# Quantizing, a norm and decay products spread over ScalarE and GpSimd in an attention, conditioning and quantized FFN kernel

## The chip, the cores and the metric

The kernel runs on one core of a Trainium2 chip. The metric is the device time in microseconds (us) of one execution. TensorE is written PE in the profile (its weight loads PEld), VectorE DVE, ScalarE ACT, GpSimd POOL and SyncE SP.

## The reference

The input x has 8 batches of 512 tokens with 256 channels, in fp32. Two blocks follow each other, both with a residual:

```python
x = x + attn(cond(x, itok), ...)
x = x + ffn(cond2(x, ...), w_gate, w_up, w_down)
```

- cond picks one of eight weight matrices per batch and applies it.
- attn is causal linear attention with 16 heads (no softmax), a gate and a layer norm.
- cond2 has a recurrence over time (causal_ema), a gate, eight decaying traces of the gated input with learned rates, which are blended, a second gate, and then the norm that this change touches:

```python
out = einsum(soma * gate, Wout)
mu, var = out.mean(-1), out.var(-1)
return (out - mu) / sqrt(var + 1e-5) * gamma + beta
```

- ffn quantizes its inputs per token to 8 bits before each of its products, and its weights to three values:

```python
scale = 127.0 / clip(max(abs(x), axis=-1), 1e-5)
xq = clip(round(x * scale), -128, 127) / scale
```

  It does this to the output of cond2 (256 channels) and to silu(gate) * up (1024 channels).

## The kernel before

**Stages.** For each batch there are three generators: attention(b), cond2(b) and ffn(b). A token tile has 128 tokens, so a batch has NT = 4 of them; C = 256 channels are KC = 2 blocks of 128. Each generator stops at yields. The list at the end of the kernel (L786 to L810) gives each a start and a step: attention b starts at b with steps of 1/14, cond2 at b + 4/3 with steps of 1/10, ffn at b + 8/3 with steps of 1/9. The part with the lowest time is traced next. So in the middle of the run, attention of one batch is interleaved with cond2 of the one or two before it and with ffn of the two or three before it. At the end only cond2 and ffn, then only ffn are left.

**Order on an engine.** The kernel is traced by the Tile framework. It gives every instruction a rank by its place in the traced program, adds the waits that data and buffers need, and decides when the kernel is built, from estimates of its own, in which order each engine gets its instructions. On the chip each engine takes its instructions in that order.

**Buffers.** A pool has a number of buffers per tag (bufs); a tile of the same tag takes the next. The function bank() at L57 hands out the PSUM banks of pool ps: four buffers, one bank each, used by nearly every product outside the attention's energies and outputs, which have pools ps_e and ps_o.

**cond2 (L555 to L685).** It transposes the attention's result (px2T, L562), makes soma, h1 and mod (L567 to L590), the gated input (L593 to L609), and the traces in four parts of two decays each (L631 to L655). Each part makes dm, the decay table times mod, on GpSimd with one instruction per token tile (L634 to L637), multiplies it with gated on TensorE into ptr (L646), and adds the results to tempT on VectorE (L652). At L665 to L685 the product with woutT goes to a bank pw (two token tiles in each), ScalarE copies it to c2 (L674), VectorE takes mean and variance of each token (L675, layer_stats), GpSimd makes 1/sqrt(var + 4 eps) (L677, layer_rstd, with a power at L186), and VectorE applies mean and gamma (L679), then 1/sqrt and beta (L682). (The factor 4: gate is kept as 1 + tanh, twice the sigmoid, and the norm takes the factor out.)

**ffn (L726 to L781).** VectorE takes the largest absolute value amax of c2 (L731), and brings c2 to its quantized form: it multiplies by inv and adds MAGIC = 1.5 x 2^23, which rounds to an integer (L738), and subtracts MAGIC again on the way to bf16 (L739, tile cq). TensorE transposes cq (L743) and ScalarE copies it out (cqT). Then, per token tile, TensorE makes gate and up in two halves of 512 (L756), ScalarE the silu (L759), VectorE the product h (L760). After a yield VectorE takes hmax (L763), h_inv and hstep (L721, L723, L766), scales and rounds h in the same two steps (L767, L769, tile hq); TensorE transposes hq (phq, L772), ScalarE copies it out (hqT, L774), TensorE multiplies with w_downT (pd, L777), VectorE adds the residual (res, L779), and SyncE's queue writes it out (L780).

Of the kernel before, what the change touches and what calls it, by code (L numbers as in the profile page):

```python
# [8 lines left out]
F32 = mybir.dt.float32  # L9
BF = mybir.dt.bfloat16  # L10
I32 = mybir.dt.int32
AF = mybir.ActivationFunctionType
ALU = mybir.AluOpType
AX = mybir.AxisListType

P = 128
EPS = 1e-5

MAGIC = 12582912.0
# [13 lines left out]
def adaln_attn_ffn_kernel(ctx: ExitStack, tc: tile.TileContext, a: dict, out: bass.AP):  # L33
    nc = tc.nc
    x = a["x"]
    B, T, C = x.shape
    NT = T // P
    KC = C // P
# [8 lines left out]
    cp = ctx.enter_context(tc.tile_pool(name="const", bufs=1))  # L47
# [3 lines left out]
    p1 = ctx.enter_context(tc.tile_pool(name="p1", bufs=1))  # L51
    p2 = ctx.enter_context(tc.tile_pool(name="p2", bufs=2))
# [13 lines left out]
    nc.vector.memset(ones, 1.0)  # L66
    minus_half = cp.tile([P, 1], F32, name="minus_half")
    nc.vector.memset(minus_half, -0.5)

    causal = cp.tile([P, 64], F32, name="causal")  # L70
    for r in range(2):
# [35 lines left out]
    def load_w(name, src, pool=cp, tag=None, eng=nc.scalar):  # L107
        rows, cols = src.shape
        t = pool.tile([P, rows // P, cols], F32, tag=tag or name, name=name)
        eng.dma_start(t, src.rearrange("(k p) n -> p k n", p=P))  # L110
        return t
# [25 lines left out]
    def chunk(t):  # L137
        return slice(t * P, (t + 1) * P)
# [38 lines left out]
    def layer_stats(src, mv_row):  # L177
        st = p3.tile([P, nc.vector.BN_STATS_DIM], F32, tag="bn", name="bn")
        nc.vector.bn_stats(st, src)
        nc.vector.bn_aggr(mv_row, st)  # L180

    def layer_rstd(mv, name):

        r = p2.tile([P, NT], F32, tag="rstd", name=name)
        nc.gpsimd.tensor_scalar(r, mv[:, :, 1], 4.0 * EPS, None, ALU.add)
        nc.gpsimd.tensor_tensor(r, r, minus_half.to_broadcast([P, NT]), ALU.pow)  # L186
        return r
# [235 lines left out]
    w = {}  # L423

    def setup_cond2():
        for n in ("wgT", "wn1T", "wsomaT", "wtempT", "woutT"):
            w[n] = load_w(n, a[n], eng=nc.gpsimd)
        for n in ("bg", "gamma_c", "beta_c"):
            w[n] = load_row(n, a[n])

# [124 lines left out]
    def cond2(b):  # L555
# [29 lines left out]
        mod = p2.tile([P, NT, D], F32, tag="mod", name=f"mod_{b}")  # L585
# [45 lines left out]
        for d in range(0, D, 2):  # L631

            dm = p2.tile([P, NT, 2, 64], F32, tag="dm", name=f"dm_{b}_{d}")
            for t in range(NT):  # L634
                nc.gpsimd.tensor_mul(  # L635
                    dm[:, t], w["decay"][:, d : d + 2], mod[:, t, d : d + 2].unsqueeze(2).to_broadcast([P, 2, 64])
                )  # L637
            for k in range(KC):

                ptr = [  # L640
                    bank(f"ptr_{b}_{k}_{d}_{r}").rearrange("p (e t n) -> p e t n", e=2, n=64) for r in range(2)
                ]
                for t in range(NT):
                    for r in range(2):
                        rows = slice(64 * r, 64 * (r + 1))
                        nc.tensor.matmul(  # L646
                            ptr[r][:, :, t, :], gated[rows, t, chunk(k)], dm[rows, t], start=True, stop=True
                        )
                for r in range(2):
                    acc = tempT[:, k, :].rearrange("p (t r n) -> p t r n", r=2, n=64)[:, :, r, :]  # L650
                    for e in range(2):
                        nc.vector.scalar_tensor_tensor(  # L652
                            acc, ptr[r][:, e], w["bw_c"][:, k, d + e : d + e + 1], acc, ALU.mult, ALU.add
                        )
            yield  # L655
# [7 lines left out]
            nc.vector.scalar_tensor_tensor(soma[:, o, :], gate, 1.0, soma[:, o, :], ALU.add, ALU.mult)  # L663
        yield
        c2 = p1.tile([P, NT, C], F32, tag="c2", name=f"c2_{b}")  # L665
        mv = p2.tile([P, NT, 2], F32, tag="mvc", name=f"mvc_{b}")
        for t in range(0, NT, 2):
            pw = bank(f"pwo_{b}_{t}").rearrange("p (t c) -> p t c", t=2)
            for u in range(2):
                for k in range(KC):  # L670
                    nc.tensor.matmul(
                        pw[:, u, :], soma[:, k, chunk(t + u)], w["woutT"][:, k, :], start=k == 0, stop=k == KC - 1
                    )
            nc.scalar.copy(c2[:, t : t + 2, :], pw)  # L674
            for u in range(2):  # L675
                layer_stats(c2[:, t + u, :], mv[:, t + u, :])
        rstd = layer_rstd(mv, f"rstd_c{b}")  # L677
        for t in range(NT):
            nc.vector.scalar_tensor_tensor(  # L679
                c2[:, t, :], c2[:, t, :], mv[:, t, 0:1], w["gamma_c"], ALU.subtract, ALU.mult  # L680
            )
            nc.vector.scalar_tensor_tensor(  # L682
                c2[:, t, :], c2[:, t, :], rstd[:, t : t + 1], w["beta_c"], ALU.mult, ALU.add
            )
        c2s[b] = c2  # L685


# [38 lines left out]
    def ffn(b):  # L726
        c2, x2 = c2s[b], x2s[b]


        amax = p2.tile([P, NT], F32, tag="amax", name=f"amax_{b}")  # L730
        nc.vector.tensor_reduce(amax, c2, AX.X, ALU.max, apply_absolute_value=True)  # L731
        inv = act_scales(amax, [P, NT], f"c_inv_{b}")
        steps = p2.tile([P, 2, NT], F32, tag="steps", name=f"steps_{b}")
        for i in range(2):
            nc.vector.tensor_scalar(steps[:, i, :], amax, w["wstep"][:, i : i + 1], None, ALU.mult)
        cq = p1.tile([P, NT, C], BF, tag="cq", name=f"cq_{b}")
        for t in range(NT):
            nc.vector.tensor_scalar(c2[:, t, :], c2[:, t, :], inv[:, t : t + 1], MAGIC, ALU.mult, ALU.add)  # L738
        nc.vector.tensor_scalar(cq, c2, -MAGIC, None, ALU.add)  # L739
        pt = bank(f"pcq_{b}", BF).rearrange("p (k n) -> p k n", k=KC)  # L740
        for k in range(KC):
            for t in range(NT):
                nc.tensor.transpose(pt[:, k, chunk(t)], cq[:, t, chunk(k)], ident_bf)  # L743
        cqT = p2.tile([P, KC, T], BF, tag="cqT", name=f"cqT_{b}")
        nc.scalar.copy(cqT, pt)
        yield

        for t in range(NT):
            h = p2.tile([P, INNER], F32, tag="h", name=f"h_{b}_{t}")
            for j in range(INNER // 512):  # L750
                cols = slice(j * 512, (j + 1) * 512)
                pgu = []
                for n in ("w_gateT", "w_upT"):
                    pm = bank(f"p{n}_{b}_{t}_{j}")
                    for k in range(KC):
                        nc.tensor.matmul(pm, cqT[:, k, chunk(t)], w[n][:, k, cols], start=k == 0, stop=k == KC - 1)  # L756
                    pgu.append(pm)
                sig = p2.tile([P, 512], F32, tag="sig", name=f"sig_{b}_{t}_{j}")
                nc.scalar.activation(sig, pgu[0], AF.Silu, scale=steps[:, 0, t : t + 1])  # L759
                nc.vector.scalar_tensor_tensor(h[:, cols], pgu[1], steps[:, 1, t : t + 1], sig, ALU.mult, ALU.mult)  # L760
            yield
            hmax = p2.tile([P, 1], F32, tag="hmax", name=f"hmax_{b}_{t}")
            nc.vector.tensor_reduce(hmax, h, AX.X, ALU.max, apply_absolute_value=True)  # L763
            hinv = act_scales(hmax, [P, 1], f"h_inv_{b}_{t}")
            hstep = p2.tile([P, 1], F32, tag="hstep", name=f"hstep_{b}_{t}")
            nc.vector.tensor_scalar(hstep, hmax, w["wstep"][:, 2:3], None, ALU.mult)  # L766
            nc.vector.tensor_scalar(h, h, hinv, MAGIC, ALU.mult, ALU.add)  # L767
            hq = p2.tile([P, INNER], BF, tag="hq", name=f"hq_{b}_{t}")
            nc.vector.tensor_scalar(hq, h, -MAGIC, None, ALU.add)  # L769
            pt = bank(f"phq_{b}_{t}", BF)  # L770
            for k in range(KI):
                nc.tensor.transpose(pt[:, chunk(k)], hq[:, chunk(k)], ident_bf)  # L772
            hqT = p2.tile([P, INNER], BF, tag="hqT", name=f"hqT_{b}_{t}")
            nc.scalar.copy(hqT, pt)  # L774
            pd = bank(f"pd_{b}_{t}")[:, :C]
            for k in range(KI):
                nc.tensor.matmul(pd, hqT[:, chunk(k)], w["w_downT"][:, k, :], start=k == 0, stop=k == KI - 1)  # L777
            res = p2.tile([P, C], F32, tag="res", name=f"res_{b}_{t}")
            nc.vector.scalar_tensor_tensor(res, pd, hstep, x2[:, t, :], ALU.mult, ALU.add)  # L779
            nc.sync.dma_start(out[b, chunk(t), :], res)  # L780
            yield  # L781
# [12 lines left out]
    while line:  # L794
        line.sort()
        at, step, b, what = line.pop(0)
# [73 lines left out]
```

## Time and profile before

| | |
|---|---|
| Time, median of three runs | 1080.57 us (1074.35 to 1085.64) |
| Profiled execution, its own time | 1082.68 us |
| Its span, first to last instruction | 1080.9 us |
| Mean granted TensorE clock | 0.88 of full speed |
| Busy: TensorE, VectorE, ScalarE, GpSimd | 849.7, 565.6, 300.9, 252.2 us |
| VectorE busy in 597 to 716 (one batch, in the middle) | 62.4 of 119 us |
| VectorE busy in 910 to 1030 (cond2 and ffn left) | 80.1 of 120 us |
| VectorE: L763, L767, L769, 32 each | 1218, 869, 755 ns |
| VectorE: L679, L682, 32 each | 471, 667 ns |
| GpSimd: dm (L635), 128 | 411 ns |

The profile shows one execution. Busy is the time in which an engine had an instruction under way. A line of the waits reads: engine, tile and line that waited, the engine, tile and line that released it, then the total in us, how often, and the longest. A line of the order of time reads: start and duration in us, engine, line, operation, written tile<-read tiles, shapes, count, and in brackets how long the engine sat idle before it and what ended that.

### The profile page before, as it was taken

To read this page: it belongs to the slowest core of one execution; us is meant where nothing else is said; L and a number is where in the kernel's file an instruction comes from. 1 tells how busy PE (TensorE), PEld (TensorE's weight loads), DVE (VectorE), ACT (ScalarE), POOL (GpSimd) and SP (SyncE) were. 2 spreads that over 40 slices of the span, in tenths; PEclk is the share of its full clock that TensorE was granted. 3 is DMA by queue.
4 is the path that set the end of the run, shared out by engine and by line. 5 is a ranking of instruction groups with operands and counts; after the bars stand their busy time and mean duration, and the time that the engine had idled before them with its cause. 6 is when DMAs were issued, how large, how long until landed. Compare 5 with 4: busy or idle time off the path is not lost.

```text
span 1080.9 us, 22096 instructions
## 1 busy us (share of the span) xinstructions
PE 849.7 (79%) x9644; PEld 573.9 (53%) x9644; DVE 565.6 (52%) x1231; ACT 300.9 (28%) x481; POOL 252.2 (23%) x379
## 2 busy tenths in 40 slices
PE   1789679799778996799968996899778995885654
PEld 0466547566555674566735674566555674543322
DVE  8724534435552845537462736446543547656743
ACT  1832131223222231234222331234122421331221
POOL 6443222223122211222123211133122211011000
PEclk9899779798986898998988998899988998888866
DMA  9000110000000000000100000000000000000000
GB/s 282 12 3 12 41 39 2 11 1 2 2 15 6 7 26 5 16 6 2 26 15 6 7 26 5 16 1 7 25 6 5 7 7 6 10 5 6 10 10 15
DMA packets 16850, 19.31 MB, mean 18 GB/s; under 512 B 3330, under 2 KB 15394, under 8 KB 16754
## 3 DMA queue, kind: packets, MB, share of 16 engines
q1 hardware_dynamic: 12418, 10.56, 3.2%
q0 software_dynamic: 2048, 5.58, 1.6%
q10 hardware_dynamic: 2288, 1.76, 0.5%
q8 instruction: 76, 1.25, 0.5%
q14 instruction: 20, 0.16, 0.1%
HBM read 13.63 MB, written 4.19 MB: 16 GB/s over the span
## 4 chain that ended last, share of the span: by engine, by line
PE 50%; DVE 18%; issue 14%; POOL 9%; ACT 8%; DMA 1%; ACTq 0%; POOLq 0%; DVEq 0%
PE po L315 6%; PE pwg L598 5%; PE pe L297 4%; DVE tempT L652 4%; POOL ktok L235 4%; PE pd L777 3%; PE ptr L646 3%; PE pso L579 3%; PE py L203 3%; PE pw_gateT L756 2%; DVE hmax L763 2%; POOL st L268 2%; PE ptg L660 2%; ACT sig L759 2%; PE phq L772 2%
## 5 line engine op out<-in xcount | busy, mean ns | idle before, releaser
L652 DVE SCALAR_TENSOR_TENSOR tempT<-ptr,bw_c,tempT 128x256 f32<-128x256 f32 x256 | 104.6, 475 | 45.4 <-PE ptr L646 45.2
L760 DVE SCALAR_TENSOR_TENSOR h<-pw_upT,steps,sig 128x512 f32<-128x512 f32 x64 | 47.2, 748 | 112.8 <-ACT sig L759 67.8
L646 PE MATMUL ptr<-dm,gated 64*128 64x128 f32 x1024 | 94.8, 319 | 7.7 <-DVE tempT L652 7.0
L646 PEld LDWEIGHTS ptr<-dm,gated 64*128 64x128 f32 x1024 | 85.2, 222 | 23.3 <-issue 19.7
L772 PE MATMUL phq<-ident_bf,hq 128*128 128x128 bf16 x256 | 26.0, 262 | 83.2 <-DVE hq L769 83.2
L216 PE MATMUL pkq<-wkq,yT 128*128 128x512 f32 x128 | 78.2, 740 | 16.2 <-DVE tempT L652 10.5
L235 POOL TENSOR_TENSOR ktok<-sg,cs 128x512 f32<-128x512 f32 x32 | 42.2, 1319 | 177.9 <-ACT sg L223 177.9
L297 PEld LDWEIGHTS pe<-qT,kT 32*64 32x64 f32 x2048 | 66.6, 136 | 29.8 <-issue 24.5
L297 PE MATMUL pe<-qT,kT 32*64 32x64 f32 x2048 | 80.2, 228 | 0.9 <-ACT qT L243 0.9
L774 ACT COPY hqT<-phq 128x1024 bf16<-128x1024 bf16 x32 | 32.4, 1013 | 156.2 <-PE phq L772 156.2
L635 POOL TENSOR_TENSOR dm<-decay,mod 128x128 f32<-128x128 f32 x128 | 48.5, 411 | 98.5 <-PE ptr L646 98.5
L772 PEld LDWEIGHTS <-hq 128*128 128x128 bf16 x256 | 20.4, 118 | 90.6 <-DVE hq L769 89.2
L777 PE MATMUL pd<-w_downT,hqT 128*128 128x256 bf16 x256 | 46.1, 341 | 19.9 <-ACT hqT L774 19.5
L759 ACT ACTIVATE sig<-pw_gateT,steps 128x512 f32<-128x512 f32 x64 | 43.2, 686 | 66.5 <-PE pw_gateT L756 65.4
L301 DVE TENSOR_TENSOR et<-pe,causal 128x512 f32<-128x512 f32 x64 | 43.8, 687 | 33.1 <-PE pe L297 32.4
L779 DVE SCALAR_TENSOR_TENSOR res<-pd,hstep,x 128x256 f32<-128x256 f32 x32 | 15.4, 481 | 87.3 <-PE pd L777 87.3
L223 ACT ACTIVATE sg<-pkq 128x512 f32<-128x512 f32 x32 | 19.1, 597 | 117.5 <-PE pkq L216 117.5
L216 PEld LDWEIGHTS pkq<-wkq,yT 128*128 128x128 f32 x128 | 26.1, 226 | 41.3 <-issue 28.7
L242 PE MATMUL pkT<-ident,ktok 128*128 128x128 f32 x128 | 21.1, 287 | 33.8 <-POOL ktok L235 33.8
L756 PEld LDWEIGHTS <-cqT 128*128 128x128 bf16 x256 | 24.5, 104 | 42.7 <-issue 20.2
L756 PE MATMUL pw_gateT<-w_gateT,cqT 128*128 128x512 bf16 x128 | 41.9, 412 | 5.9 <-ACT sig L759 2.4
L268 POOL TENSOR_TENSOR st<-total,own 128x256 f32<-128x256 f32 x56 | 40.6, 749 | 23.4 <-DVE total L278 17.5
(222 smaller groups left out, 1610.9 us busy)
## 6 DMA issues: line engine op xcount, KB each, us to landing
x<-in_x_dram SPq DMA_DIRECT2D x8, 512.0 KB
out_dram<-res SPq DMA_DIRECT2D x32, 128.0 KB
wt<-in_weightT_dram SPq DMA_DIRECT2D x8, 256.0 KB
bw<-in_blend_dram POOLq DMA_DIRECT2D x2, 512.0 KB, 6.1
w_gateT_raw<-in_w_gateT_dram POOLq DMA_DIRECT2D x2, 512.0 KB, 7.3
w_upT_raw<-in_w_upT_dram POOLq DMA_DIRECT2D x2, 512.0 KB, 4.2
w_downT_raw<-in_w_downT_dram POOLq DMA_DIRECT2D x2, 512.0 KB, 4.7
wgT<-in_wgT_dram POOLq DMA_DIRECT2D x1, 512.0 KB, 6.8
```

The costliest lines, as they stand in the source:

```text
L216: nc.tensor.matmul(pkq, yT[:, k, chunk(t)], wkq[:, k].rearrange("p e c -> p (e c)"), start=k == 0, stop=k == KC - 1)
L235: nc.gpsimd.tensor_mul(tok.rearrange("p (h e d) -> p h e d", e=2, d=HD), sg[:, i].unsqueeze(2).to_broadcast([P, H, 2, HD]), cs[:, t, :].re ...
L268: nc.gpsimd.tensor_mul(sts[c], total[0].rearrange("p (g f) -> p g f", g=NG).unsqueeze(2).to_broadcast([P, NG, 2, 2 * HD]), own.rearrange(" ...
L297: nc.tensor.matmul(pe[64 * r : 64 * (r + 1), g, u, :], kT[rows, g, at], qT[rows, g, at], start=True, stop=True)
L315: nc.tensor.matmul(po[q : q + 32, r, half, u, :], *factors, start=(r, q) not in begun, stop=last)
L598: nc.tensor.matmul(pwg[:, u, :], src[:, k % KC, chunk(t + u)], w["wgT"][:, k, :], start=k == 0, stop=k == 2 * KC - 1,)
L646: nc.tensor.matmul(ptr[r][:, :, t, :], gated[rows, t, chunk(k)], dm[rows, t], start=True, stop=True)
L652: nc.vector.scalar_tensor_tensor(acc, ptr[r][:, e], w["bw_c"][:, k, d + e : d + e + 1], acc, ALU.mult, ALU.add)
L756: nc.tensor.matmul(pm, cqT[:, k, chunk(t)], w[n][:, k, cols], start=k == 0, stop=k == KC - 1)
L759: nc.scalar.activation(sig, pgu[0], AF.Silu, scale=steps[:, 0, t : t + 1])
L772: nc.tensor.transpose(pt[:, chunk(k)], hq[:, chunk(k)], ident_bf)
L777: nc.tensor.matmul(pd, hqT[:, chunk(k)], w["w_downT"][:, k, :], start=k == 0, stop=k == KI - 1)
```

## The change

- In setup, the mean of each row of woutT over its 256 outputs is subtracted from it, so that the product with it has mean zero over the channels.
- In cond2's last part ScalarE squares pw and sums each token's squares (accum_out). The copy to c2, the statistics and the subtraction of the mean go. GpSimd makes rstd from the sums. VectorE multiplies pw, still in PSUM, by rstd and gamma into c2. GpSimd adds beta, for two token tiles at once.
- In ffn the scaling with MAGIC goes from VectorE to ScalarE (Identity with scale and bias as per-partition pointers), for c2 and for h; the subtraction of MAGIC with the cast to bf16 goes from VectorE to GpSimd.
- The four dm products of a part become one instruction on GpSimd.

```diff
+    magic = cp.tile([P, 1], F32, name="magic")
+    nc.vector.memset(magic, MAGIC)
...
+        means = p1.tile([P, KC], F32, tag="means", name="means")
+        nc.vector.tensor_reduce(means, w["woutT"], AX.X, ALU.add)
+        nc.vector.tensor_scalar(means, means, 1.0 / C, None, ALU.mult)
+        for k in range(KC):
+            nc.vector.tensor_scalar(w["woutT"][:, k, :], w["woutT"][:, k, :], means[:, k : k + 1], None, ALU.subtract)
...
-            for t in range(NT):
-                nc.gpsimd.tensor_mul(
-                    dm[:, t], w["decay"][:, d : d + 2], mod[:, t, d : d + 2].unsqueeze(2).to_broadcast([P, 2, 64])
-                )
+            nc.gpsimd.tensor_mul(
+                dm,
+                w["decay"][:, d : d + 2].unsqueeze(1).to_broadcast([P, NT, 2, 64]),
+                mod[:, :, d : d + 2].unsqueeze(3).to_broadcast([P, NT, 2, 64]),
+            )
...
-        mv = p2.tile([P, NT, 2], F32, tag="mvc", name=f"mvc_{b}")
+        squares = p2.tile([P, NT], F32, tag="squares", name=f"squares_{b}")
+        pws = []
...
-            nc.scalar.copy(c2[:, t : t + 2, :], pw)
-            for u in range(2):
-                layer_stats(c2[:, t + u, :], mv[:, t + u, :])
-        rstd = layer_rstd(mv, f"rstd_c{b}")
+                square = p1.tile([P, C], F32, tag="square", name=f"square_{b}_{t + u}")
+                nc.scalar.activation(square, pw[:, u, :], AF.Square, accum_out=squares[:, t + u : t + u + 1])
+            pws.append(pw)
+
+        rstd = p2.tile([P, NT], F32, tag="rstd", name=f"rstd_c{b}")
+        nc.gpsimd.tensor_scalar(rstd, squares, 1.0 / C, 4.0 * EPS, ALU.mult, ALU.add)
+        nc.gpsimd.tensor_tensor(rstd, rstd, minus_half.to_broadcast([P, NT]), ALU.pow)
         for t in range(NT):
             nc.vector.scalar_tensor_tensor(
-                c2[:, t, :], c2[:, t, :], mv[:, t, 0:1], w["gamma_c"], ALU.subtract, ALU.mult
+                c2[:, t, :], pws[t // 2][:, t % 2, :], rstd[:, t : t + 1], w["gamma_c"], ALU.mult, ALU.mult
             )
-            nc.vector.scalar_tensor_tensor(
-                c2[:, t, :], c2[:, t, :], rstd[:, t : t + 1], w["beta_c"], ALU.mult, ALU.add
-            )
+            if t % 2:
+                nc.gpsimd.tensor_add(
+                    c2[:, t - 1 : t + 1, :],
+                    c2[:, t - 1 : t + 1, :],
+                    w["beta_c"].unsqueeze(1).to_broadcast([P, 2, C]),
+                )
...
-            nc.vector.tensor_scalar(c2[:, t, :], c2[:, t, :], inv[:, t : t + 1], MAGIC, ALU.mult, ALU.add)
-        nc.vector.tensor_scalar(cq, c2, -MAGIC, None, ALU.add)
+            nc.scalar.activation(c2[:, t, :], c2[:, t, :], AF.Identity, bias=magic, scale=inv[:, t : t + 1])
+        nc.gpsimd.tensor_scalar(cq, c2, -MAGIC, None, ALU.add)
...
-            nc.vector.tensor_scalar(h, h, hinv, MAGIC, ALU.mult, ALU.add)
+            nc.scalar.activation(h, h, AF.Identity, bias=magic, scale=hinv)
...
-            nc.vector.tensor_scalar(hq, h, -MAGIC, None, ALU.add)
+            nc.gpsimd.tensor_scalar(hq, h, -MAGIC, None, ALU.add)
```

## Prediction

> **What bounds the kernel now.** I read the page's busy shares, then the waits of TensorE, then the order of time around the longest of them.
>
> ```profile
> PE 849.7 (79%) x9644; PEld 573.9 (53%) x9644; DVE 565.6 (52%) x1231; ACT 300.9 (28%) x481; POOL 252.2 (23%) x379
> ```
>
> TensorE is the busiest. The change takes work from VectorE (52%) and gives it to two engines with much room. That helps only where TensorE waits for VectorE. Its waits (total us, times, longest):
>
> ```profile
> PE phq L772 <- DVE hq L769: 83.2, 16, 8.9
> PE pkT L242 <- POOL ktok L235: 33.8, 32, 2.5
> ...
> PE pd L777 <- ACT hqT L774: 19.5, 20, 1.1
> ...
> PE pkq L216 <- DVE tempT L652: 10.5, 12, 1.3
> ...
> PE pkq L216 <- DVE res L779: 2.9, 3, 1.0
> ```
>
> The largest wait by far is for hq, the very product that moves. Six of its 16 are 6.96 us each, one per batch at 299.75, 424.98, 547.18, 666.13, 785.09 and 903.95; ten lie in the drain after 910. Is it a wait for VectorE's load, or for a chain? The last one, in order of time:
>
> ```profile
> 1070.11 1.22 DVE L763 TENSOR_REDUCE hmax<-h 128x1 f32<-128x1024 f32 x1
> 1071.36 0.15 DVE L721 TENSOR_SCALAR hmax<-hmax 128x1 f32<-128x1 f32 x1
> 1071.55 0.17 DVE L723 RECIPROCAL h_inv<-hmax 128x1 f32<-128x1 f32 x1
> 1071.63 0.20 DVE L766 TENSOR_SCALAR hstep<-hmax,wstep 128x1 f32<-128x1 f32 x1
> 1071.75 0.75 DVE L767 TENSOR_SCALAR h<-h,h_inv 128x1024 f32<-128x1024 f32 x1
> 1072.54 0.69 DVE L769 TENSOR_SCALAR hq<-h 128x1024 bf16<-128x1024 f32 x1
> ...
> 1073.29 1.04 PE L772 MATMUL phq<-ident_bf,hq 128*128 128x128 bf16 x8 [4.29 <-DVE hq L769]
> ```
>
> It is a chain: scale and round take 1.53 us from 1071.75 to 1073.28, and nothing else is in flight. At the six others VectorE is behind: at 666 its queue ran without a pause from 654.43.
>
> ```profile
> 659.08 2.80 DVE L652 SCALAR_TENSOR_TENSOR tempT<-ptr,bw_c,tempT 128x256 f32<-128x256 f32 x7
> ...
> 661.80 0.91 DVE L416 SCALAR_TENSOR_TENSOR x<-og,rstd_a,x 128x256 f32<-128x256 f32 x2
> ...
> 664.22 0.14 DVE L721 TENSOR_SCALAR hmax<-hmax 128x1 f32<-128x1 f32 x1
> ...
> 666.13 1.03 PE L772 MATMUL phq<-ident_bf,hq 128*128 128x128 bf16 x8 [6.96 <-DVE hq L769]
> ```
>
> But what stands ahead of the quantizing there (eight tempT, then x and og of the first norm) is not touched by the change; only the last 1.5 us is. TensorE doesn't fill the hole: tiles of the four-buffer PSUM pool reach it in program order everywhere I looked, and phq and pd come before the next ptr.
>
> [...] 686 ns for a 128x512 with one (L759), 597 without (L223). [...] The trace has two-input rows (1024 elements 2349 ns, L206), and no large one-input row with a read. [...] L769 mostly takes 694 ns, once 1659. [...]
>
> **The change part by part.**
>
> h, 32 times. Leaves VectorE: 869+755 ns mean, 1.53 us as a clean chain. On ScalarE: L539 is 1048 ns for 1024 SBUF elements without pointers, plus 2 x 89 = 1.23 us. On GpSimd: a four-element TENSOR_SCALAR is 245 ns (L185); affine selects of 64 and 128 elements take 233 and 283, so 0.78 ns per element; the 1024 memset is 1154. That gives 1.0 to 1.3; I take 1.15. Upper bound: the two-input 2.35. Two hand-overs at 0.05 (hq's end to phq). Sum 1.23+1.15+0.10 = 2.48, against 1.53: **+0.95 us per h**. Exposed: 15 of the 16 waits (that at 1026.78 is below), and the one at 955.74, where hq ended as TensorE did: 16 x 0.95 = **+15.2**. The other 16 have slack (1.4 us at 634.41, 5 at 605, 8 at 688) that covers it; at a two-input rate the first would show too. Queued behind the waiting scale on ScalarE are copies out of PSUM; at 655 to 667 ScalarE had none to do, and in the drain everything hangs on the same chain. Behind hq on GpSimd stand dm and ktok. dm is ready at 662 and used at 670; ktok needs a later pkq.
>
> c2's quantizing, 8 times: 4 x 0.34 + 0.69 = 2.1 us becomes 4 x 0.51 (two pointers at 256, back to back) + 1.15 = 3.2. pcq ran at 645.8 while cq ended at 619.2: hidden by 26 us, except in the last batch.
>
> Second norm, 8 times. Gone: two copies of 585, four statistics of 418+172, four L679 of 471, four L682 of 667. Added: four squares at 372 to 690 (256 PSUM copy, L232; up to two extras), four PSUM products at 481 (L779), two GpSimd adds at 1.32 (L235's size). Pow stays 1.04. VectorE loses 6.9-1.9 = 5 us per batch; with h (6.5) and c2 (1.9) some 13 of its 62. New wait: pw's two banks are held past squares, pow and two products, to about 608.7 and 609.5 instead of 604.1 and 605.8 in the batch of 601. px2T at 607.65 then comes 1.1 us late, covered by energies, while the wait of pkq for res (0.96 us, three times) goes, since res no longer queues behind eight products. I net these to **0**, with 0 to +1 per batch as bounds. If Square needed its own table: 1.28 us per load, beside TensorE's work, 0 to +5 in all.
>
> Last batch, 1015 to 1027. VectorE's queue is the wait here (8.94 us). Squares end about 1015.9, rstd 1017.5, products 1019.4; the second gate matmul needs pw's bank and slips to 1018.5, its up to 1019.4; h 1020.9, hmax 1022.1, scale 1023.8, hq 1025.0 instead of 1026.7: **-1.8**.
>
> dm, 32 fused from 128: 4 x 0.41 in a row took 1.47 us; a 512-element one is 1.32 to 1.61 (L235, L483): **0**, used 8 us later.
>
> Setup: centring woutT on VectorE, a 128x512 reduce (0.6), a small one, two of 0.34, about 1.5 us in a stretch where VectorE is 74% busy (44.7 of the first 60 us): **+0.5**. The reduce also waits for woutT's transfer (6.8 us from issue to landing); behind it stands btemp's row, which ran at 24.37 after transfers that GpSimd issues later, so the wait adds nothing. No transfer is added or moved on any queue. magic: one memset of 59 ns (as L68), nothing.
>
> Sum: 15.2-1.8+0.5 = +13.9. The profiled execution took 1082.68 (span 1080.9): 1096.6. It lies 2.1 above the median of the runs, 1080.57, so **1095**.
>
> **The rivals.**
>
> B, GpSimd is the bound of the chain: a rounding pass at the two-input rate. Then each h adds 1.2 more: 16 x 1.2 = 19, plus six slots at 634's place with 0.8: 24; time 1119. For: every large GpSimd row with reads runs at 2.3 to 2.6 ns per element. Against: the affine selects' 0.78.
>
> C, the change doesn't do more than move: VectorE's relief brings hmax forward as much as the two hops push hq back. [...] Then 16 x 0 - 1.8: about 1080, within 1%. Against: what precedes hmax at the six stops stays.
>
> D, the other side: at the six stops and at 921, 980 and 997 VectorE does eight tempT (3.2 us) or the x and og rows (2.6) between hmax's reduce and its small rows, because the planner ranks them first. With scale and rounding gone from VectorE's estimates the order is made anew; if the small rows come ahead at all nine, 9 x 3 = 27 us go: 1095-27 = 1068. It decides from five stops on (13.9/3). Against: ranks follow the program's order, which doesn't change.
>
> **How the numbers follow.** A (this forecast) 0.40, its own range 1088 to 1106, of which 0.32 is slower by over 1% and 0.08 within (1% is about what a measurement of this kernel can tell from no change; the limits are 1069.8 and 1091.4). B 0.10, slower. C 0.22, within. D 0.28, faster. So faster 0.28, same 0.30, slower 0.42. The range leaves out half of D's lower side and B's upper side: 1058 to 1120.
>
> **What would show it.** Right: phq waits for GpSimd; the six stops are about 7.9 us instead of 6.96; the last chain's hinv to phq takes 2.5 us instead of 1.5; VectorE falls to about 460 busy, ScalarE rises to about 360, GpSimd to about 315; TensorE's busy time is unchanged. Wrong: a rounding row far from 1.15 us (A to B); stops that shrink, or the small rows of hmax directly behind its reduce (C or D); table loads beside Square; matmuls of pwo or px2T that wait for squares or products for more than 1 us per batch.

## The result and the profile after

The changed kernel takes 1183.24 us (median of four runs, 1180.98 to 1187.19); the kernel before took 1077.46 beside it. The ratio is 1.102, interval 1.093 to 1.111: slower by a tenth. The profiled execution has 1183.58 us of its own and a span of 1181.9, at a mean TensorE clock of 0.856 instead of 0.880.

The engines' busy times, from the first part of the page:

```profile
PE 868.5 (73%) x9644; PEld 583.9 (49%) x9644; DVE 478.2 (40%) x1036; ACT 359.7 (30%) x593; POOL 364.5 (31%) x339
```

VectorE lost 87 us (the forecast had some 105) and ScalarE gained 59, as forecast. GpSimd has 50 us more than forecast, and TensorE, whose work is untouched, is busy 18.8 us longer with the same 9644 instructions. The waits of TensorE say where the time is (total us, times, longest):

```profile
PE phq L788 <- POOL hq L785: 146.6, 25, 9.5
PE pkT L244 <- POOL ktok L237: 39.4, 32, 2.8
...
PE pd L793 <- ACT hqT L790: 22.6, 22, 1.5
...
PE px2T L570 <- DVE res L795: 1.5, 2, 0.8
```

The wait for hq grew from 83.2 us in 16 stops to 146.6 in 25. All listed waits of TensorE together grew by 82.5 (225.6 to 308.1). With the 18.8 of busy time that makes 101.3, where the span grew by 101.0. So 63.4 us are hq's own, 5.6 are ktok's, 18.8 are longer busy time of TensorE, and the other 13.5 are small waits. The last h, in order of time (start, duration):

```profile
1170.18 0.16 DVE L739 RECIPROCAL h_inv<-hmax 128x1 f32<-128x1 f32 x1
...
1170.44 1.24 ACT L783 ACTIVATE h<-h,magic,h_inv 128x1024 f32<-128x1024 f32 x1 [2.52 <-DVE h_inv L739]
1171.76 2.77 POOL L785 TENSOR_SCALAR hq<-h 128x1024 bf16<-128x1024 f32 x1 [10.86 <-ACT h L783]
1174.58 1.03 PE L788 MATMUL phq<-ident_bf,hq 128*128 128x128 bf16 x8 [7.02 <-POOL hq L785]
```

The scale takes 1.24 us, as forecast (1.23). The rounding takes 2.77, not 1.15. From the end of h_inv to phq are now 4.24 us, where they were 1.57 in the last h of the kernel before. The six long stops, one per batch, went from 6.96 to 9.54 us.

### The profile page after: what moved, and what is told of

Same layout as the page of the kernel before. It is cut to its first block, busy times and chain, and to the rows that moved or that the text cites. A ratio compares the mean times of both kernels' runs of the same rounds, so it can differ in the third digit from the quotient of the medians.

```text
span 1181.9 us, 22025 instructions
## 1 busy us (share of the span) xinstructions
PE 868.5 (73%) x9644; PEld 583.9 (49%) x9644; DVE 478.2 (40%) x1036; ACT 359.7 (30%) x593; POOL 364.5 (31%) x339
## 4 chain that ended last, share of the span: by engine, by line
PE 44%; POOL 17%; issue 14%; DVE 13%; ACT 10%; DMA 1%; POOLq 0%; ACTq 0%; DVEq 0%
POOL hq L785 6%; PE po L317 4%; PE pe L299 3%; POOL ktok L237 3%; PE pd L793 3%; PE ptr L655 3%; DVE tempT L661 3%; PE pwg L606 3%; PE pwo L681 3%; PE py L205 2%; PE pso L587 2%; PE pw_gateT L772 2%; POOL st L270 2%; PE phq L788 2%; DVE hmax L779 2%
## 5 line engine op out<-in xcount | busy, mean ns | idle before, releaser
L785 POOL TENSOR_SCALAR hq<-h 128x1024 bf16<-128x1024 f32 x32 | 88.7, 2772 | 164.6 <-ACT h L783 164.6
L788 PE MATMUL phq<-ident_bf,hq 128*128 128x128 bf16 x256 | 28.1, 272 | 148.3 <-POOL hq L785 146.6
L655 PE MATMUL ptr<-dm,gated 64*128 64x128 f32 x1024 | 100.3, 333 | 7.4 <-DVE tempT L661 6.8
L655 PEld LDWEIGHTS ptr<-dm,gated 64*128 64x128 f32 x1024 | 90.5, 236 | 23.1 <-issue 17.7
L793 PE MATMUL pd<-w_downT,hqT 128*128 128x256 bf16 x256 | 51.5, 368 | 22.7 <-ACT hqT L790 22.6
L783 ACT ACTIVATE h<-h,magic,h_inv 128x1024 f32<-128x1024 f32 x32 | 39.6, 1237 | 88.7 <-DVE h_inv L739 88.7
L642 POOL TENSOR_TENSOR dm<-decay,mod 128x512 f32<-128x512 f32 x32 | 34.1, 1075 | 74.9 <-PE ptr L655 74.9
L793 PEld LDWEIGHTS <-hqT 128*128 128x128 bf16 x256 | 29.5, 126 | 38.7 <-ACT hqT L790 29.1
```

What stands on the lines that cost most here:

```text
L655: nc.tensor.matmul(ptr[r][:, :, t, :], gated[rows, t, chunk(k)], dm[rows, t], start=True, stop=True)
L785: nc.gpsimd.tensor_scalar(hq, h, -MAGIC, None, ALU.add)
```

## The experiments

Each time stands beside the kernel before on the same chip; ratios have their 95% interval. Line numbers are those of each kernel. Edits are against the changed kernel where nothing else is said.

### Which part costs: four kernels

Theory R: the length of h's chain sets the end, and the rounding row is why. Rival N: the second norm, which holds two PSUM banks for longer. Rival Q: other work that stands behind the roundings in GpSimd's queue. The first kernel takes only the rounding of h back to VectorE:

```diff
-            nc.gpsimd.tensor_scalar(hq, h, -MAGIC, None, ALU.add)
+            nc.vector.tensor_scalar(hq, h, -MAGIC, None, ALU.add)
```

> The changed kernel with one line back: hq's rounding on VectorE; all else (scale on ScalarE, cq on GpSimd, norm, dm) stays. Theory R (the slowdown is h's chain, and its rounding row of 2.77 us on GpSimd): the chain from h_inv to phq falls from 4.15 to 1.24 + 0.69 + 0.1 = 2.0 us, so 2.1 us on 25 to 32 exposed h: 1105 to 1120. Theory N (pw's banks held by squares, power and products): hardly changes, above 1160. Theory Q (GpSimd's queue: cq and hq ahead of ktok, dm and st): about 1130, because cq still stands in that queue.

Measured: 1120.53 us, ratio 1.033 (1.029 to 1.037). The six long stops are 7.40. This one instruction gives back 63 us; the time lies at R's upper end (1120) and far below N's 1160.

The second keeps the centred norm, the squares and the one dm product, and takes both scales and both roundings back to VectorE:

```diff
-            nc.scalar.activation(c2[:, t, :], c2[:, t, :], AF.Identity, bias=magic, scale=inv[:, t : t + 1])
-        nc.gpsimd.tensor_scalar(cq, c2, -MAGIC, None, ALU.add)
+            nc.vector.tensor_scalar(c2[:, t, :], c2[:, t, :], inv[:, t : t + 1], MAGIC, ALU.mult, ALU.add)
+        nc.vector.tensor_scalar(cq, c2, -MAGIC, None, ALU.add)
...
-            nc.scalar.activation(h, h, AF.Identity, bias=magic, scale=hinv)
+            nc.vector.tensor_scalar(h, h, hinv, MAGIC, ALU.mult, ALU.add)
...
-            nc.gpsimd.tensor_scalar(hq, h, -MAGIC, None, ALU.add)
+            nc.vector.tensor_scalar(hq, h, -MAGIC, None, ALU.add)
```

> The changed kernel with both steps of quantizing, of c2 and of h, back on VectorE; norm by squares, beta on GpSimd, centred weights and one dm stay. R: what is left of the change is harmless or a small gain, 1065 to 1085. N: 1150 or more. Q: 1070 to 1090, as R.

Measured: 1083.57, ratio 1.002 (1.000 to 1.004). Norm and dm together come to nothing: N falls, and the 25 us of work that VectorE lost here (565.6 to 540.6) brought no gain.

The third is the kernel before with only hq's rounding on GpSimd:

```diff
-            nc.vector.tensor_scalar(hq, h, -MAGIC, None, ALU.add)
+            nc.gpsimd.tensor_scalar(hq, h, -MAGIC, None, ALU.add)
```

> The kernel before with one line moved: hq's rounding on GpSimd, the scale stays on VectorE. R: the chain is 0.78 + 2.77 + 0.1 = 3.65 instead of 1.53 us, +2.1 for 25 to 30 h: 1130 to 1145. N: within 1% of before. Q: 1110 to 1140, too near to R to tell apart here.

The fourth is the kernel before with a mere delay between scale and rounding, on an engine that has room; the copies change no value:

```diff
             nc.vector.tensor_scalar(h, h, hinv, MAGIC, ALU.mult, ALU.add)
+            nc.scalar.copy(h, h)
+            nc.scalar.copy(h, h)
```

> The kernel before with two copies of h onto itself on ScalarE between scale and rounding (both on VectorE): 2 x 1.05 + 0.1 = about 2.1 us more in each h's chain, and nothing more on GpSimd. R (the length of the chain alone sets the time): as the kernel before with hq's rounding on GpSimd, 1125 to 1145. Q (GpSimd's queue): under 1100, since GpSimd's queue is as before. N: as before.

Measured: 1131.47, ratio 1.045 (1.042 to 1.047), and 1128.30, ratio 1.042 (1.040 to 1.045). The first line of TensorE's waits in the third kernel, then in the fourth:

```profile
PE phq L772 <- POOL hq L769: 123.5, 23, 10.1
```

```profile
PE phq L774 <- DVE hq L771: 115.1, 22, 9.4
```

The long stops are 9.10 and 9.13 us. It makes nearly no difference whether GpSimd rounds or ScalarE dawdles, so for hq it is not GpSimd's queue (Q had under 1100 us for the fourth): what counts is the length of the chain. About 2.15 us per h cost 45 to 48 us, so 21 to 22 us of run time per us of chain. Of that, hq's own waits are 40.3 us in the third kernel and 31.9 in the fourth, because stops that had slack before are now exposed: 23 and 22 instead of 16.

### The rest: c2's rounding and the scales

With hq's rounding back on VectorE 37 us remained, while h's chain was only half a us longer than before. Two kernels part this. Rival S, here: the scales on ScalarE hold up the copies out of PSUM behind them. One takes both roundings back and leaves both scales on ScalarE:

```diff
-        nc.gpsimd.tensor_scalar(cq, c2, -MAGIC, None, ALU.add)
+        nc.vector.tensor_scalar(cq, c2, -MAGIC, None, ALU.add)
...
-            nc.gpsimd.tensor_scalar(hq, h, -MAGIC, None, ALU.add)
+            nc.vector.tensor_scalar(hq, h, -MAGIC, None, ALU.add)
```

> The changed kernel with both roundings (hq and cq) back on VectorE; both scales stay on ScalarE. With hq's rounding alone back the kernel stood 37 us above the one before, though h's chain is then only 0.5 us longer (about 11 us at the 21 to 23 us that each us of chain has cost). Theory Q (cq's rounding of 2.78 us on GpSimd stands ahead of ktok, which TensorE's pkT waits for): the wait of pkT for ktok falls back to about 34 us in all, a batch in the steady part back to 120 or 121 us, the time to 1092 to 1100 us. Rival S (the scales on ScalarE delay the copies out of PSUM): the time stays at 1112 to 1120 us and the steady batches at 126 us.

The other leaves c2's part as changed, and takes scale and rounding of h back:

```diff
-            nc.scalar.activation(h, h, AF.Identity, bias=magic, scale=hinv)
+            nc.vector.tensor_scalar(h, h, hinv, MAGIC, ALU.mult, ALU.add)
...
-            nc.gpsimd.tensor_scalar(hq, h, -MAGIC, None, ALU.add)
+            nc.vector.tensor_scalar(hq, h, -MAGIC, None, ALU.add)
```

> The changed kernel with h wholly on VectorE (scale and rounding), and c2's scale on ScalarE and cq's rounding on GpSimd as changed. Theory Q: the wait of pkT for ktok rises above 2 us once per batch, a steady batch takes 124 to 126 us, the time is 1100 to 1110 us. Rival S (it is the scale of h on ScalarE that costs, through the chain and the copies queued behind it): the time is within 5 us of the kernel before, 1078 to 1089 us. A third, T: both halves of c2's path are hidden until the last batch, which has 3.6 us more of it: 1087 us.

Measured: 1101.79, ratio 1.017 (1.013 to 1.022), and 1102.21, ratio 1.018 (1.014 to 1.022). Set in a ladder, the medians are 1083.6 (norm and dm alone), 1102.2 (with c2's part), 1120.5 (with h's scale), 1183.2 (with h's rounding): 18.6, 18.3 and 62.7 us. Each is good to some us only: the kernel before, measured beside them, had medians from 1077.5 to 1083.5. Taking cq's rounding away from the 1120.5 saves 18.7, so c2's rounding is about the whole of c2's part. (This takes it that the parts add up, as the ladder does.) Q is right about c2's half, though its 1092 to 1100 for the first kernel was missed by 2 us, and T is wrong: the stop in the last batch is 7.93 us, as without c2's part. S's numbers were missed in both kernels, but it isn't wholly wrong, as a second view below shows. Where c2's cost lies, in the changed kernel's order of time in one batch:

```profile
638.03 2.78 POOL L755 TENSOR_SCALAR cq<-c 128x1024 bf16<-128x1024 f32 x1 [4.82 <-ACT c L754]
640.78 1.27 POOL L237 TENSOR_TENSOR ktok<-sg,cs 128x512 f32<-128x512 f32 x1
...
642.11 1.11 PE L244 MATMUL pkT<-ident,ktok 128*128 128x128 f32 x4 [2.21 <-POOL ktok L237]
```

Nobody waits for cq itself, but ktok stands behind it in GpSimd's queue, and TensorE waits for ktok. The stop is only 2.2 us, and in the kernel before it was 0.97 at this place (614.85). What follows it is dearer. Busy time of TensorE, its instructions and its granted clock in stretches of 4 us, the changed kernel (then DMA share and GB/s):

```profile
637.00:641.00 4.00, 2.39 (x36) 0.99 0.01 2
641.00:645.00 4.00, 2.89 (x40) 0.50 0.00 0
645.00:649.00 4.00, 4.00 (x8) 0.66 0.00 0
...
665.00:669.00 4.00, 3.94 (x46) 0.50 0.00 0
669.00:673.00 4.00, 4.00 (x84) 0.67 0.16 43
...
773.00:777.00 4.00, 1.78 (x42) 1.00 0.00 0
...
797.00:801.00 4.00, 4.00 (x107) 1.00 0.07 5
```

After the stop for ktok, and again after the new stop of 2.98 us for hq at 665, the clock is at half for some 6 us; pkT's four transposes take 1.11 us there and 0.66 elsewhere. Half clock does not follow every such stop. Three batches of the changed kernel have the same two stops, 2.2 us for ktok and 3.0 for hq. After those at 642, 665, 904 and 927 the clock was at 0.50; after those at 775 and 796 it stayed at 1.00. What decides between the two is not shown. The batch of the latter two took 127.9 us (701.9 to 829.8), the others 133.4 and 134.7. So such a drop cost, by an estimate from these times, about 3 us, as much again as the stop itself. (The clean pair is 127.9 and 133.4, 2.8 us per drop; the third batch has more half clock elsewhere too, at 859 and 893.)

The scales have a queue as well. Once in the middle of the changed kernel ScalarE stands idle for 3.83 us with c2's scale at the head of its queue, which waits for c_inv; the copy vz, whose product was done at 504.8, is behind it, and TensorE waits for vz:

```profile
508.42 0.60 ACT L754 ACTIVATE c<-c,magic,c_inv 128x256 f32<-128x256 f32 x1 [3.83 <-DVE c_inv L739]
508.93 0.35 ACT L234 COPY vz<-pv 128x256 f32<-128x256 f32 x1
509.33 1.08 PE L252 MATMUL pst<-vz,ktok 64*64 64x32 f32 x32 [2.68 <-ACT vz L234]
```

A second such stop, for soma behind c2's scale, is 2.3 to 2.6 us long, in the last part. All kernels with c2's scale on ScalarE have both, about 5 us of waits; the kernel before and the one with norm and dm alone have neither. So S is right in kind, and c2's scale isn't free, though the ladder is too coarse to show it.

### The row by itself

Rows on GpSimd at the very end of the kernel before, each twice, among them:

```diff
+        nc.gpsimd.tensor_scalar(qb, src, -0.5, None, ALU.add)
+        nc.gpsimd.tensor_scalar(qf, src, -0.5, None, ALU.add)
+        nc.gpsimd.tensor_copy(qc, src)
+        nc.gpsimd.tensor_tensor(qt, src, half_c.to_broadcast([P, INNER]), ALU.subtract)
+        nc.gpsimd.tensor_scalar(q2, src, 2.0, -0.5, ALU.mult, ALU.add)
```

> The kernel before with GpSimd rows added at its very end, each twice, 128 partitions, nothing beside them: add of a constant from fp32 to bf16 (1024 and 512 elements), the same to fp32, copies to bf16 and fp32, a subtraction of a broadcast operand to bf16, a multiply and add to bf16. Theory G1 (the cast to bf16 is what made 2.77 us of an expected 1.15): the rows to fp32 take 1.0 to 1.3 us and those to bf16 2.8. Rival G2 (tensor_scalar itself runs at 2.7 ns per element on GpSimd, whatever it writes): add to fp32 takes 2.8 too, the copies less. Rival G3 (2.77 us is contention with VectorE in the run): without other work the row takes 1.0 to 1.6 us.

The groups of instructions, by shape (busy us, then mean ns of one, then idle before):

```profile
L818 POOL TENSOR_SCALAR probe_add_bf<-probe_src 128x1024 bf16<-128x1024 f32 x2 | 5.6, 2778 | 51.3 <-DVE probe_src L813 51.3
L820 POOL TENSOR_SCALAR probe_add_f<-probe_src 128x1024 f32<-128x1024 f32 x2 | 5.5, 2768 | 1.4 <-DVE hq L769 1.4
L828 POOL TENSOR_TENSOR probe_tt_bf<-probe_src,half_c 128x1024 bf16<-128x1024 f32 x2 | 3.8, 1884 | 0.0
L822 POOL TENSOR_SCALAR probe_add_bf<-probe_src 128x512 bf16<-128x512 f32 x2 | 3.0, 1483 | 0.0
L830 POOL TENSOR_SCALAR probe_two_bf<-probe_src 128x1024 bf16<-128x1024 f32 x2 | 2.1, 1036 | 0.0
L824 POOL CAST probe_copy_bf<-probe_src 128x1024 bf16<-128x1024 f32 x2 | 2.1, 1032 | 0.0
```

With nothing beside it the row takes 2.78 us, to fp32 as to bf16: contention (G3) and the cast (G1) are out. G2 is right only for the form with one operation: (2778 - 1483)/512 = 2.5 ns per element. The same instruction with two operations takes 1.04 us, like a cast. The slow form is the one that leaves the second operation out. (Only an addition was tried alone; whether a single multiplication is as slow was not tested.)

### The change as it was priced

So both roundings are written with two operations; nothing else differs from the changed kernel:

```diff
-        nc.gpsimd.tensor_scalar(cq, c2, -MAGIC, None, ALU.add)
+        nc.gpsimd.tensor_scalar(cq, c2, 1.0, -MAGIC, ALU.mult, ALU.add)
...
-            nc.gpsimd.tensor_scalar(hq, h, -MAGIC, None, ALU.add)
+            nc.gpsimd.tensor_scalar(hq, h, 1.0, -MAGIC, ALU.mult, ALU.add)
```

> The changed kernel with one thing different: both roundings on GpSimd are written with two operations (times 1.0, then minus MAGIC) instead of one with the second left out. By itself that row took 1.04 us against 2.78 for the one-operation row. So this is the change as the prediction had priced it (1.15 us). Theory P (only the price of the row was wrong in the prediction, the rest of its sum stands): the stops are 7.8 to 7.9 us, the time 1090 to 1098 us. Rival K (a longer chain costs more than its own length, because TensorE's clock falls to 0.5 after each new stop, as the 63 us between the changed kernel and the one with hq's rounding on VectorE say for 2.1 us): h's part comes back by 1.74/2.1 of 63, 52 us, and cq's by 1.74/2.1 of 19, 16 us, so 1110 to 1120 us.

Measured: 1118.02, ratio 1.032 (1.028 to 1.036). Its waits:

```profile
PE phq L788 <- POOL hq L785: 97.4, 19, 7.8
...
PE pd L793 <- ACT hqT L790: 23.6, 22, 1.8
```

This is the cleanest test of the forecast's sum. The stops are 7.81, as it said, and hq's waits grew by 14.2 us (97.4 less 83.2), where it said 15.2, or 13.4 with the 1.8 gained in the last batch. Yet the time is 35 us up, not 14: of the span's 37.0 us, hq's waits are 14.2, the two stops behind c2's scale 5.0, longer busy time of TensorE 4.6, the wait of pd for hqT 4.1, and the rest small waits. Theory P falls and K's number stands, but K's reason, the clock, is at most a small part of it here. The mean clock of the profiled execution is 0.881, that of the kernel before 0.880. In the four batches from 429 to 926 it is 0.91 and TensorE was busy for 411.5 us; in those of the kernel before, 425 to 904, 0.92 and 404.1.

### Shorter instead of longer

If the chain's length costs 21 us per us, a shorter one should pay. In the kernel before, hmax by halves beside the two halves of h, scale and rounding by halves, hstep behind them:

```diff
+                nc.vector.tensor_reduce(hmax2[:, j : j + 1], h[:, cols], AX.X, ALU.max, apply_absolute_value=True)
...
-            nc.vector.tensor_reduce(hmax, h, AX.X, ALU.max, apply_absolute_value=True)
+            nc.vector.tensor_tensor(hmax, hmax2[:, 0:1], hmax2[:, 1:2], ALU.max)
...
+            for j in range(2):
+                cols = slice(j * 512, (j + 1) * 512)
+                nc.vector.tensor_scalar(h[:, cols], h[:, cols], hinv, MAGIC, ALU.mult, ALU.add)
+                nc.vector.tensor_scalar(hq[:, cols], h[:, cols], -MAGIC, None, ALU.add)
```

> The kernel before with a shorter chain from h to its transposes, all on VectorE: hmax is reduced by halves (the first while the second half of gate and up is multiplied), hstep is made after the rounding, and scale and rounding go in two halves, so that the first four transposes of phq start after the first. From the rows of before: reduce 1.22 to about 0.70 with the join, hstep off the chain 0.06, first half of scale and rounding about 0.85 instead of 1.53: about 1.25 us less per h. Theory R (the length of h's chain sets the end, with 21 to 23 us of time per us when it is made longer): the stops fall from 6.96 to about 5.7 us and the time by 15 to 28 us, to 1055 to 1068 us. Rival V (only lengthening costs; below the present length another wait ends last, or VectorE's four added rows per h delay others): within 5 us of before.

Measured: 1081.72, ratio 0.999 (0.997 to 1.001). V's number, but the reason is in the trace of a long stop:

```profile
410.49 0.69 DVE L762 TENSOR_REDUCE hmax<-h 128x1 f32<-128x512 f32 x1
...
412.95 2.80 DVE L652 SCALAR_TENSOR_TENSOR tempT<-ptr,bw_c,tempT 128x256 f32<-128x256 f32 x7
...
418.11 0.15 DVE L765 TENSOR_TENSOR hmax<-hmax 128x1 f32<-128x1 f32 x1
...
418.67 0.88 DVE L770 TENSOR_SCALAR h<-h,h_inv 128x512 f32<-128x512 f32 x2
...
419.95 1.03 PE L776 MATMUL phq<-ident_bf,hq 128*128 128x128 bf16 x8 [6.90 <-DVE hq L771]
```

The halves of hmax are done at 411.2, and the next row of h's chain starts at 418.11: VectorE has tempT and the first norm's rows in between. The saved part of the reduce was never on the path there. Behind it both scales were put ahead of the first rounding (0.88 us together) and the joining row cost 0.18, so the tail was 1.84 us instead of 1.91. The kernel thus did not shorten what ends the long stops, and so is no evidence against R there. In the last part the stops did get shorter (the longest from 8.94 to 7.05; hq's waits as a whole fell from 83.2 to 77.5), and why the time shows nothing of that stays open.

### The order instead of the length

What stands between hmax and its small rows is the other parts' work, traced after the yield. This kernel is the one before with that yield moved; no instruction is added or removed:

```diff
-            yield
             hmax = p2.tile([P, 1], F32, tag="hmax", name=f"hmax_{b}_{t}")
...
             nc.vector.tensor_scalar(hq, h, -MAGIC, None, ALU.add)
+            yield
             pt = bank(f"phq_{b}_{t}", BF)
```

> The kernel before with the yield between h and hmax moved to behind hq, so that hmax, h_inv, scale and rounding are traced right after h, ahead of what the other parts bring in between; no instruction is added or taken away. Theory O (the six long stops of TensorE come from VectorE's order: hmax is done 7 us before h_inv starts, because the attention's norm stands between them; the length of h's rows counts only behind that): the stops of 6.96 us vanish or fall below 3 us, the norm and what follows it come 1.7 us later, and the time falls by 20 to 45 us, to 1037 to 1062 us. Rival W (the norm of attention is what the order serves: its delay stops TensorE elsewhere by as much, or the planner sets the same order again): 1075 to 1090 us.

Measured: 1042.71, ratio 0.962 (0.958 to 0.967). A steady stop in its order of time:

```profile
754.47 1.22 DVE L762 TENSOR_REDUCE hmax<-h 128x1 f32<-128x1024 f32 x1
...
755.93 0.15 DVE L721 TENSOR_SCALAR hmax<-hmax 128x1 f32<-128x1 f32 x1
...
757.52 0.67 DVE L768 TENSOR_SCALAR hq<-h 128x1024 bf16<-128x1024 f32 x1
...
759.89 0.77 PE L772 MATMUL phq<-ident_bf,hq 128*128 128x128 bf16 x8 [2.27 <-DVE tempT L652]
```

hq is done at 758.2, and TensorE waits only 2.27 us, for tempT to set a PSUM bank free. A steady batch takes 114 us instead of 119, at a clock of 0.96 instead of 0.93. So theory O holds, and with it comes a test: here hq has 1.7 us to spare in the steady part. Both cures together, two-operation roundings and the moved yield in the changed kernel:

> The changed kernel with two-operation roundings on GpSimd and the yield moved behind hq. With the yield moved in the kernel before, TensorE's transposes of phq no longer waited for hq in the middle of the run but for a PSUM bank that tempT set free, with hq done 1.7 us earlier; only the last two batches still wait for hq. Theory L (a longer chain costs only where hq is what ends last): the 0.85 us is then covered in the six steady stops and costs in the last part alone, some 13 to 18 us above the kernel with only the yield moved, so 1054 to 1064 us. Rival M (the spread costs 35 us wherever the yield is, by ScalarE's and GpSimd's queues and the clock): 1073 to 1083 us.

Measured: 1059.16, ratio 0.979 (0.973 to 0.985), in L's range. The six steady stops are 1.33 us, and none waits for hq. The same spread that cost 35 us costs 16.5 here (1059.16 less 1042.71; the kernel before beside them took 1083.70 and 1082.83). The last part, from the sixth steady stop to the end (us, TensorE's busy time and instructions, clock, DMA share, GB/s), with the moved yield alone and then with the spread:

```profile
874.49:1042.80 168.31, 110.39 (x640) 0.79 0.03 10
```

```profile
876.01:1058.00 181.99, 111.72 (x640) 0.79 0.03 9
```

So 13.7 of the 15.2 us by which the two spans differ lie in the last part, where L had put them. That it is the longer chain which is paid there is not shown: hq's waits as a whole grew by only 1.4 us (36.6 to 38.0). The waits of pd for hqT grew by 3.5, and the two stops behind c2's scale are there again with 5.0. Finally the moved yield with the shorter chain:

> The kernel before with both the yield moved behind hq and h's chain shortened on VectorE (hmax by halves, scale and rounding by halves). By itself the shortening was worth nothing measurable: the six steady stops stayed at 6.90 us because they began behind the attention's norm, and only the last stops fell by 0.66 us. Theory L: with the yield moved the steady stops end with tempT, so the shortening again counts only in the last part, 10 stops of 0.4 to 0.7 us, 4 to 7 us: 1035 to 1040 us. Rival M2 (the shortening's added rows delay tempT, which is what ends the stops now): 1042 to 1050 us.

Measured: 1049.22 (1035.05 to 1053.71, five runs), ratio 0.970 (0.967 to 0.974). No gain over the moved yield alone (1042.71, measured on another chip) is shown. The executions spread widely: the profiled one, 1035.05, had a clock of 0.92 and lies in L's range, the other four took 1048.38 to 1053.71 at 0.892 to 0.905. In the profiled one the stops for hq fell by 2.2 us in all, and those for ktok grew by 3.8. The median fits M2, its reason (a delayed tempT) does not: those waits of phq and pkq fell by 3.5 us. The trace is of the fastest execution, so what the others lost isn't seen in it, and the cause stays open.

## Why the prediction was wrong

The direction of the likeliest case was right and its place too: hq, its chain, the six stops. The size was wrong, 1095 against 1183, outside the range. Of the 88 us between, 65 went away when the rounding rows were written in the form that takes the forecast time (1183.24 less 1118.02); the other 23 remain with the row as priced. By its steps:

**The rounding row: the step that failed.** "That gives 1.0 to 1.3; I take 1.15. Upper bound: the two-input 2.35." It took 2.772 us, above the upper bound. The price came from affine selects at 0.78 ns per element, another operation, and the only one-operation TENSOR_SCALAR rows in the trace, L185, had four elements, where 245 ns say nothing of a slope. The upper bound took it that a large row of one input, of which that trace has none, is no slower than the two-input L206 of 2349 ns. The probe shows otherwise for this form: one input in 2.78 us, a row with a second, broadcast operand in 1.88, the two-operation form in 1.04. With the true row the chain is 2.6 us longer, not 0.95. Rival B had the mechanism, and its 2.35 us was still too low; that its time of 1119 is near the 1118 of the kernel with the fast form is a coincidence.

**Sixteen exposed stops: too few for the true length.** The other slots had slack "1.4 us at 634.41". With 2.6 us more that is gone, and 25 stops are exposed. With the row as priced (1.04 us) there are 19, three of them new and short, and the sum of the waits was right within 1 us.

**A us of waiting is a us of time: the second step that failed.** "TensorE's busy time is unchanged" took for granted that a stop costs its own length. It was wrong even with the row as priced: 14.2 us more for hq, 35 us in all. TensorE's own busy time rose by 4.6 us there and by 18.8 in the changed kernel. The half clock is shown in the changed kernel after four of six like stops, by the estimate above about 3 us each, and the two stops behind c2's scale, 5.0 us; what makes the other small waits longer was not measured apart. The prediction never asked what a stop does to the work behind it.

**c2's quantizing, "hidden by 26 us".** pcq was hidden; ktok behind cq in GpSimd's queue was not. The prediction asked who stands behind hq on GpSimd, not who stands behind cq, nor behind c2's scale on ScalarE (vz and soma). Cost: 18.6 us. With the two-operation cq the stop for ktok at that place is down to 0.48 us; how much of the 18.6 goes with it was not measured apart.

**h's scale on ScalarE** was priced rightly: 1.23 forecast, 1.237 measured. (The 89 ns that the forecast put on each pointer operand are the difference of two Silu rows of 128x512 in the kernel before, 686 ns with such an operand at L759 and 597 without at L223.) c2's scales took 0.60 and then three in 1.58, for 4 x 0.51. The stops grew by 0.48 us with it (6.92 to 7.40), and it cost about 18 us of time, of which hq's waits are 8.0 (82.1 to 90.1): once more the second failed step. What the rest is stays open.

**Second norm and dm: 0**, and 1.002 (1.000 to 1.004) was measured. Square (385 ns and 196 for reading its sum, inside 372 to 690) needed no table loads (28 in all, before and after), products took 476 for 481, adds 1326 for 1320, the fused dm 1075 for 1320 to 1610. Of the waits of pwo for a square that the forecast had in mind, the kernel with norm and dm alone has two, 0.5 us in all. pkq's wait for res went, 2.9 us, and px2T waits 1.5 us for it instead. The last stop fell from 8.94 to 7.92 with VectorE's rounding, for the forecast 1.8; in the changed kernel it is 9.34. Setup's 0.5 us is below what these runs can tell.

**A misreading.** Before the change L769 took 1.66 us twice (at 320.46 and 446.02), not once; nothing rests on it.

**Rivals C and D.** Relief of VectorE brought nothing: the stops' order stayed. D saw what the stops are made of, eight tempT and the first norm between hmax's reduce and its small rows, but the change left that order as it was. When the order is changed by itself it pays 40 us, more than D's 27.

## What to carry to other kernels

Price a moved row by a row of its own kind and size, or carry the range beyond the nearest kin; a shape at four elements has no slope. Before work goes to an idle engine, list what is queued behind it there, for every row moved and on every engine that gets one. When the longest stop of the bound engine ends with a short chain that began late, look for what stands ahead of it: here the order, moved by one line, was worth 40 us, while spreading the load cost 106.

## What the runs showed of the hardware

In the rows by themselves, GpSimd's TENSOR_SCALAR with one operation, an addition, took 1483 ns at 512 elements per partition and 2778 at 1024, so 2.5 ns per element between the two; with two operations it took 1036 ns at 1024, a cast 1032, a copy 1030. In the changed kernel each of the 32 squares on ScalarE came with an ACTIVATION_READ_ACCUMULATOR of 196 ns. In three like batches there, of six stops of TensorE of 2.2 and 3.0 us, four were followed by some 6 us at a clock of 0.50 and two by none (1.00), with the same instructions around them. A copy on ScalarE whose source was done at 504.8 ran at 508.9, behind a scale that waited.
